# A graph attention kernel: fewer transfers before the first pass, another VectorE order for two blocks, one ScalarE table

The chip is a Trainium2. The program runs on one core of it. The metric is device time in microseconds (us), the median of several executions; executions of one kernel on one chip spread by 3 to 13 us, and by 26 us in the one batch in which two patterns of step 0 are mixed (below).

## The reference, cut to what matters

Two layers work on 4096 nodes with 256 features. Layer 0 is graph attention with four heads; layer 1 takes two steps of top-p attention beside two hops over a dense normalized matrix.

```python
# layer 0
h = jnp.maximum(_layernorm(x), 0.0)
h = (h @ W).reshape(n, heads, head_dim)
e = src[:, :, None] + dst.T[None, :, :]          # src, dst: projections of h per head
e = jnp.where(e > 0, e, ALPHA * e)               # leaky
e = jnp.where(adj[:, None, :] > 0, e, NEG_INF)
out = jnp.einsum('nhm,mhd->nhd', softmax(e), h)  # then a layer norm, and x = x + ...
# layer 1, cut
for n in range(2):
    A = _top_p_attention(Xa, W1, W2, W3)         # softmax, keep the top 0.9 of the mass, renormalize
    Xf = R @ Xf                                  # R = S + I, rows normalized
    Xa = A @ Xa
    Z = Z + Xf @ U1[n].T + Xa @ U2[n].T
```

## The kernel before

Layer 0 starts with a prologue of 32 blocks of 128 nodes. Each block is normalized (`hb`), transposed on TensorE (`tp`, `hT`), multiplied by the weights (`mm`), weighted by two exponentials (`uv`), and split into three bfloat16 parts (`parts`), which go out to DRAM for the later passes. Beside this, GpSimd's queue loads the edges of the first pass. Then 16 passes over pairs of blocks follow, each with sign, masks and products.

```python
            for g in range(NB // 4):
                ...
                rs, nmr = steps(mv, 4, rows)                       # four small GpSimd operations
                for i in range(4):
                    b = 4 * g + i
                    hb = rows.tile([P, D], F32, name="hb")
                    nc.scalar.activation(hb, x4[:, i, :], AF.Relu, scale=rs[:, i:i + 1], bias=nmr[:, i:i + 1])
                    pt = ps2.tile([P, KC, P], F32, name="tp")
                    for k in range(KC):
                        nc.tensor.transpose(pt[:, k, :], hb[:, ts(k, P)], ident)
                    hT = rows.tile([P, KC, P], F32, name="hT")
                    nc.scalar.copy(hT, pt)
                    ...  # two matmuls into pm, two exponentials, two products into uv
                    parts = rows.tile([P, H, 2, W3 + 1], BF16, name="parts", bufs=6)
                    set1 = nc.gpsimd.memset(parts[:, :, :, W3:], 1.0)
                    nc.scalar.copy(parts[:, :, :, :W1], uv)
                    nc.vector.tensor_tensor(uv, uv, parts[:, :, :, :W1], ALU.subtract)
                    if b % 3 == 2 and len(ax) < NB // 4:
                        with tc.issue_after(set1.ins):
                            ax.append(edges(0, len(ax)))           # GpSimd's queue, a load of 1 MB
                    nc.scalar.copy(parts[:, :, :, ds(W1, W1)], uv)
                    nc.vector.tensor_tensor(parts[:, :, :, ds(2 * W1, W1)], uv, parts[:, :, :, ds(W1, W1)], ALU.subtract)
                    nc.gpsimd.tensor_copy(ut0[b // QUARTER][:, b % QUARTER], parts[:, 0])
                    nc.scalar.dma_start(uv_d[:, :, b].rearrange("h p t w -> p h t w"), parts)
            ...
            def signs(k, p):
                g = l0m.tile([P, 2, G0 * P], BF16, name="g", bufs=4)
                ...  # ACT: Relu(BIG * sr + d_big), one per block of the pair
```

In layer 1, each step of attention finds its cut by probes. A probe is a VectorE instruction over 128x4096 that ends in one number per row; a chain of small GpSimd operations on 128x1 turns that number into the next probe's threshold (`lowered`).

```python
            def chosen_kept(b):
                r = blocks[b]
                if 0 < b < NB - 1:
                    second_probe(blocks[b + 1])
                candidates(r, found)
                if b == 0:
                    masked(r)
                ...
                if b + 2 < NB:
                    first_step(blocks[b + 2])
                if b == 0:
                    second_probe(blocks[1])
                if b + 1 < NB:
                    third_probe(blocks[b + 1])
                ...
                if b > 0:
                    masked(r)
```

## Time and profile before

| | kernel before |
|---|---|
| timed executions | 3261.56 us median (3259.44 to 3265.22) |
| the profiled execution | 3278.61 us |
| first row write issued | 31.46 us |
| last row write issued | 143.91 us |
| first sign (start of pass 0) | 151.07 us |
| first masked block of step 0 | 1546.4 us |
| first masked block of step 1 | 2449.4 us |

The profiled execution was 17 us longer than the timed ones. A table of such times, stage by stage, is the way to read a program that is one serial sequence of full stages: a stage that starts earlier passes its gain on unless the next gives it back.

The waits from 27 to 143 us (engine, what waited, for what: us in total, times, longest).

```profile
POOL parts L212 <- DMA uv_d<-parts: 58.1, 17, 7.1
...
ACT parts L218 <- DMA adj_d<-ax: 18.0, 2, 10.4
```

GpSimd waits for row writes to land before it may set the column of ones of a buffer that is used again. ACT is held twice, 18.0 us in all, by writes of edges. The prediction takes a shared semaphore for the reason, and the semaphores recorded in the packed trace agree: the row write issued at 110.40 and an edge write that landed at 110.32 use the same one, and so do the row write issued at 129.25 and an edge write that landed at 129.15.

### The profile page before, as it was taken

To read this page: it belongs to the slowest core of one execution; us is meant where nothing else is said; L and a number is where in the kernel's file an instruction comes from. 1 tells how busy PE (TensorE), PEld (TensorE's weight loads), DVE (VectorE), ACT (ScalarE), POOL (GpSimd) and SP (SyncE) were. 2 spreads that over 40 slices of the span, in tenths; PEclk is the share of its full clock that TensorE was granted. 3 is DMA by queue.
4 is the path that set the end of the run, shared out by engine and by line. 5 is a ranking of instruction groups with operands and counts; after the bars stand their busy time and mean duration, and the time that the engine had idled before them with its cause. 6 is when DMAs were issued, how large, how long until landed. Compare 5 with 4: busy or idle time off the path is not lost. (4 is left out here: it accounts for less than half of the span.)

```text
span 3276.4 us, 51761 instructions
## 1 busy us (share of the span) xinstructions
PE 2973.4 (91%) x19213; PEld 2417.6 (74%) x19213; DVE 2656.6 (81%) x5020; ACT 1952.7 (60%) x2903; POOL 1266.9 (39%) x1793
## 2 busy tenths in 40 slices
PE   4499899898989999986899999999879999999996
PEld 2299799797977888874677777777757777777785
DVE  6598899998976555546999999999469988888894
ACT  5588687786862110016577776775266777776742
POOL 3200100201000000003798998899015656656530
PEclk8699999999999999997899999999889999999998
DMA  9825639356225555520000000000100000000000
GB/s 260 228 83 144 204 113 255 117 142 206 73 85 181 165 177 164 161 89 1 10 19 15 16 20 15 15 18 17 62 13 10 25 20 25 22 22 25 20 27 13
DMA packets 198314, 268.48 MB, mean 82 GB/s; under 512 B 13728, under 2 KB 155552, under 8 KB 198048
## 3 DMA queue, kind: packets, MB, share of 16 engines
q1 hardware_dynamic: 152272, 207.99, 19.4%
q0 software_dynamic: 16896, 33.56, 5.7%
q10 hardware_dynamic: 28880, 23.48, 2.3%
q8 instruction: 155, 2.54, 0.3%
q14 instruction: 111, 0.91, 0.1%
HBM read 226.77 MB, written 71.76 MB: 91 GB/s over the span
## 5 line engine op out<-in xcount | busy, mean ns | idle before, releaser
L799 PE MATMUL acc<-X,eT 128*128 128x256 f32 x4160 | 978.4, 381 | 0.8 <-ACT eT L793 0.8
L799 PEld LDWEIGHTS acc<-X,eT 128*128 128x128 f32 x4160 | 762.6, 191 | 90.1 <-ACT eT L793 1.9
L291 PE MATMUL acc<-ut,m 128*128 128x195 bf16 (+1 forms) x8192 | 732.2, 249 | 82.3 <-DVE m L279 49.7
L291 PEld LDWEIGHTS <-m 128*128 128x128 bf16 x8192 | 703.4, 98 | 111.1 <-DVE m L279 66.9
L272 ACT ACTIVATE g<-sr,d_big 128x1024 bf16<-128x1024 f32 x512 | 550.6, 1178 | 50.2 <-DVE m L278 40.6
L618 ACT ACTIVATE void<-e,c 128x2048 int8<-128x2048 f32 x244 | 490.4, 2010 | 0.6
L611 ACT ACTIVATE e<-mm,nm 128x1024 f32<-128x1024 f32 x256 | 285.9, 1117 | 341.2 <-PE mm L488 338.1
L432 PE MATMUL racc<-hl,ar 128*128 128x512 f32 x2048 | 469.4, 391 | 16.8 <-issue 10.0
L432 PEld LDWEIGHTS racc<-hl,ar 128*128 128x128 f32 x2048 | 384.5, 188 | 101.5 <-issue 10.8
L791 PEld LDWEIGHTS tp<-ident,e 128*128 128x128 f32 x2080 | 246.8, 143 | 224.2 <-issue 126.6
L793 ACT COPY eT<-tp 128x512 f32<-128x512 f32 x520 | 303.4, 584 | 168.9 <-PE tp L791 168.1
L791 PE MATMUL tp<-ident,e 128*128 128x128 f32 x2080 | 327.9, 281 | 57.0 <-DVE e L728 42.8
L278 DVE TENSOR_TENSOR m<-g,ax 128x2048 bf16<-128x2048 bf16 x256 | 311.7, 1218 | 41.8 <-ACT g L272 38.8
L707 DVE MAX8 cand<-big 128x8 f32<-128x228 f32 (+1 forms) x1088 | 343.9, 395 | 0.1
L279 DVE TENSOR_TENSOR m<-ax,m 128x2048 bf16<-128x2048 bf16 x256 | 317.1, 1239 | 26.9 <-DVE m L278 1.4
L488 PE MATMUL mm<-kT,qT 64*128 64x512 f32 x1024 | 304.8, 678 | 33.5 <-ACT e L611 33.5
L428 DVE CAST ar<-at 128x1024 fp32r<-128x1024 bf16 x256 | 177.0, 692 | 169.8 <-PE racc L432 167.3
L694 DVE SCALAR_TENSOR_TENSOR big<-e,lowered 128x4096 f32<-128x4096 f32 x64 | 286.8, 4482 | 20.9 <-POOL lowered L639 20.9
L728 DVE SCALAR_TENSOR_TENSOR e<-e,found 128x4096 f32<-128x4096 f32 x64 | 286.7, 4480 | 0.0
L443 ACT ACTIVATE xf<-xf,rinv 128x256 f32<-128x256 f32 x64 | 32.7, 510 | 373.3 <-DVE xf L442 373.3
L648 POOL TENSOR_TENSOR sums<-sums 128x4 f32<-128x4 f32 (+1 forms) x64 | 106.4, 1662 | 378.8 <-ACT void L618 231.1
L488 PEld LDWEIGHTS mm<-kT,qT 64*128 64x128 f32 x1024 | 84.3, 196 | 130.6 <-issue 66.7
(245 smaller groups left out, 3269.4 us busy)
## 6 DMA issues: line engine op xcount, KB each, us to landing
at<-adj_d SPq DMA_DIRECT2D x256, 256.0 KB, 3.0
ut<-uv_d SPq DMA_DIRECT2D x60, 784.0 KB, 4.3
ax<-in_adj_t_dram POOLq DMA_DIRECT2D x32, 1024.0 KB, 13.6
adj_d<-ax SPq DMA_DIRECT2D x32, 1024.0 KB, 11.5
uv_d<-parts ACTq DMA_DIRECT2D x32, 392.0 KB, 8.2
xf<-xf_d SPq DMA_DIRECT2D x65, 128.0 KB, 2.0
sr<-s_d SPq DMA_DIRECT2D x16, 512.0 KB, 4.7
xf_d<-xf ACTq DMA_DIRECT2D x64, 128.0 KB, 2.4
```

Source lines behind the costliest of these rows:

```text
L272: nc.scalar.activation(g[:, c, :], shared[k].sr, AF.Relu, scale=BIG, bias=d_big[:, h, j:j + 1])
L278: nc.vector.tensor_tensor(m[0], g, a, ALU.min)
L279: nc.vector.tensor_tensor(m[1], a, m[0], ALU.subtract)
L291: nc.tensor.matmul(shared[k].acc[i][:, t, :cols], m[t][:, c, ts(i, P)], shared[k].ut[j // QUARTER][:, j % QUARTER, t, :cols], start=(j == ...
L432: nc.tensor.matmul(acc[i].rearrange("p s d -> p (s d)"), ar[:, c, ts(i, P)], hl[hop][:, j].rearrange("p s d -> p (s d)"), start=(j == 0), ...
L488: nc.tensor.matmul(pm[:, h, :], q[ts(h, DA), :], kT[ts(h, DA), ts(c, 512)], start=True, stop=True)
L618: nc.scalar.activation(void, r.e[:, ts(h, N // 2)], (AF.Relu, AF.Sign)[i], bias=r.c1, scale=-1.0, accum_out=r.sums[:, h, 2 + i:3 + i])
L694: nc.vector.scalar_tensor_tensor(big, r.e, r.c3, r.e, ALU.is_le, ALU.mult, accum_out=r.L)
L707: nc.vector.max(cand[:, s, :], big[:, edges[s]:edges[s + 1]])
L791: nc.tensor.transpose(pt[:, i, :], r.e[:, ts(4 * g + i, P)], ident)
L793: nc.scalar.copy(eT, pt)
L799: nc.tensor.matmul(r.acc[:, 0, :], eT[:, i, :], cur[:, j, :], start=(j == 0), stop=(j == NB - 1))
```

## The change

The intent is to move less by DMA before the first pass, to fill an idle stretch of VectorE at the start of step 0, and to load one ScalarE table for all functions in use.

```diff
+    nc.scalar.preload_act_table_set("natural_log_exp_and_others")
...
+        sr0 = l0.tile([P, G0 * P], F32, name="sr0")
...
-                    if b % 3 == 2 and len(ax) < NB // 4:
+                    if b % 6 == 5:
                         with tc.issue_after(set1.ins):
                             ax.append(edges(0, len(ax)))
...
-                    nc.scalar.dma_start(uv_d[:, :, b].rearrange("h p t w -> p h t w"), parts)
+                    nc.scalar.dma_start(uv_d[1:, :, b].rearrange("h p t w -> p h t w"), parts[:, 1:])
+                    if b % 4 == 3 and b < G0:
+                        pm = ps2.tile([P, 512], F32, name="mm", bufs=3)
+                        for i in range(4):
+                            nc.tensor.transpose(pm[:, ts(i, P)], s_c[:, 0, ds(b - 3 + i, 1)].to_broadcast([P, P]), ident)
+                        nc.scalar.copy(sr0[:, ds((b - 3) * P, 4 * P)], pm)
...
+                if len(ax) < NB // 4:          # after the first masks: the late edge loads
+                    now = small.tile([P, 1], BF16, name="now", bufs=1)
+                    seen = nc.gpsimd.tensor_copy(now, m[0][:, 0, :1])
+                    with tc.issue_after(seen.ins):
+                        while len(ax) < NB // 4:
+                            ax.append(edges(0, len(ax)))
...
-                        sources(0)
-                        shared[0].ut = ut0
+                        shared[0] = SimpleNamespace(sr=sr0, ut=ut0)
...
+                    if k == 0 and p % 4 == 1:
+                        nc.sync.dma_start(uv_d[0, :, ts(p // 4, QUARTER)], ut0[p // 4])
...
-                if 0 < b < NB - 1:
+                early = b < (1 if last else 2)
+                if not early and b < NB - 1:
                     second_probe(blocks[b + 1])
-                candidates(r, found)
-                if b == 0:
+                candidates(r, found, (lambda: second_probe(blocks[b + 1])) if early else None)
+                if early:
                     masked(r)
...
-                if b == 0:
-                    second_probe(blocks[1])
...
-                if b > 0:
+                if not early:
                     masked(r)
```

`candidates` calls its new argument between its sixteen maximum instructions and the small ones after them.

More of the change, by code (lines that the diff above doesn't have):

```diff
@@ L694, in third_probe, with candidates @@
         nc.vector.scalar_tensor_tensor(big, r.e, r.c3, r.e, ALU.is_le, ALU.mult, accum_out=r.L)
-    def candidates(r, found):
+    def candidates(r, found, between=None):
         t, after, eighth = (x[:, r.b:r.b + 1] for x in found)
@@ L707, in candidates @@
             nc.vector.max(cand[:, s, :], big[:, edges[s]:edges[s + 1]])
+        if between:
+            between()
         nc.vector.tensor_scalar(cum[:, :1], r.z, 1.0 - TOP_P, r.L, ALU.mult, ALU.subtract)
```

## The prediction

> **What bounds the kernel now.** I read the page first (busy shares, then the forty slices), then the timeline and the DMA view of the first 160 us, then the waits there, then the timelines where each step of the second layer starts.
>
> From the page, engines and slices (one slice is 81.9 us):
>
> ```profile
> PE 2973.4 (91%) x19213; PEld 2417.6 (74%) x19213; DVE 2656.6 (81%) x5020; ACT 1952.7 (60%) x2903; POOL 1266.9 (39%) x1793
> ...
> PE   4499899898989999986899999999879999999996
> ...
> DMA  9825639356225555520000000000100000000000
> ```
>
> PE is at 8 or 9 tenths nearly everywhere, but at 4 in the first two slices, where DMA is at 9 and 8. So the run is one serial sequence of full stages behind a prologue of some 150 us that does not fill PE. A microsecond saved there is saved at the end.
>
> The timeline of the prologue's end, ACT, DVE and PE (start, duration, what, idle before and its releaser):
>
> ```profile
> 110.81 0.62 ACT L218 CAST parts<-uv 128x520 bf16<-128x520 f32 x1 [10.44 <-DMA adj_d<-ax]
> ...
> 129.66 0.62 ACT L218 CAST parts<-uv 128x520 bf16<-128x520 f32 x1 [7.58 <-DMA adj_d<-ax]
> ...
> 143.91 0.37 ACTq L221 DMA_DIRECT2D uv_d<-parts  x1
> 151.07 29.22 ACT L272 ACTIVATE g<-sr,d_big 128x1024 bf16<-128x1024 f32 x28 [7.82 <-DMA uv_d<-parts]
> 153.34 1.23 DVE L278 TENSOR_TENSOR m<-g,ax 128x2048 bf16<-128x2048 bf16 x1 [9.51 <-ACT g L272]
> ```
>
> Three things are to be seen. ACT is held 10.4 and 7.6 us because its write of a block's rows (uv_d<-parts) shares a completion semaphore with a 1 MB write of edges (adj_d<-ax). The edge writes belong to pass 1 but are issued as soon as a load lands. The last write of rows goes out at 143.91. The first sign ACTIVATE waits until 151.07 **for that write to land**, since its buffer lies where `parts` was. The broadcast row `sr` is not the last thing it waits for: it was issued at 141.2 and such loads took 4.3 to 6.4 us here.
>
> The DMA view from 0 to 151 us (queue, packets, MB, share of sixteen engines):
>
> ```profile
> q0 software_dynamic: 4752, 9.44, 35.3%
> q1 hardware_dynamic: 10976, 17.47, 34.6%
> q10 hardware_dynamic: 17520, 12.99, 28.7%
> ...
> uv_d<-parts ACTq DMA_DIRECT2D x32, 392.0 KB, 8.2
> ax<-in_adj_t_dram POOLq DMA_DIRECT2D x9, 1024.0 KB, 12.7
> adj_d<-ax SPq DMA_DIRECT2D x9, 1024.0 KB, 9.6
> ```
>
> Shares sum to 98.6%, 149 us of work in 151 us: the DMA engines are the prologue's bound. Nine edge loads cost 0.353*151/9 = 5.9 us each, 32 row writes 0.287*151/32 = 1.35 us each.
>
> [...] row writes land after a median 8.2 us under this load, 2.8 us at best. [...] The trace has five loads of 1283 ns. [...] a 0.26 us POOL operation takes 3.99 us behind the 4.48 us probe (second fence below).
>
> **The change, part by part.**
>
> *Prologue DMA.* The instruction order of the changed kernel, as built, has five edge loads before the first sign instead of nine; the other three of pass 0 and the first of the next group follow the first mask. Edge writes issued before then fall from nine to about four and a half. Row writes carry three heads of four; head 0 goes out from the resident `ut` in four 0.8 MB writes, three of them before pass 0. From 40 to 130 us q1 moved 8.37 MB at 25.8% of 90 us, 2.77 us per MB, so 2.9 us per edge write and 2.2 us per `ut` write. Sum: loads -4*5.9 = -23.7, edge writes -4.5*2.9 = -13, rows -0.25*43.3 = -10.8, head 0 +3*2.2 = +6.7: **-41 us of 149**. About 108 us of DMA work remains.
>
> *What then bounds the prologue.* ACT and the chain per block. ACT has hb 0.60, hT 0.37, two exponents 0.23, two casts 1.27 and the DMA issue 0.37; back to back these overlap a little, some 2.55 us a block. The first row write is issued at 31.46, so the 32nd can't be before 31.5 + 31*2.55 = 110.5. Before, the first 22 took 31.46 to 97.43, 3.14 us a block; at that pace with no long holds it would be 128.8. Lighter DMA shortens the landing of row writes, on which the six `parts` buffers turn (POOL's memset waited 58 us for them). I choose 2.8 us a block: 118. The last row write still shares a semaphore with the fifth edge write (I count 0 to 5 us, take 1.5), and the first sign still waits for it to land (three quarters the size, fewer neighbours: 4.5 instead of 7.2). First sign at about 124 against 151.07: **-27 us**. `sr0` made by PE adds eight transposes and two copies (about 1.2 us of ACT, inside this) and, as `sr` wasn't last, gains nothing by itself.
>
> *Pass 0.* It runs at 2.7 us a pair on PE. Late loads are issued near 127 and cost 5.9 us each plus edge writes between them: landed by about 135, 143 and 152. Masks 10, 12 and 14 want them near 152, 157 and 163. No wait, with little room on the last: +0.5.
>
> *One table.* The timeline of step 1's start:
>
> ```profile
> 2413.58 1.28 ACT L554 ACT_TABLE_LOAD   x1 [1.35 <-DVE thr L570]
> 2414.87 0.26 ACT L554 ACTIVATE roots<-roots 128x64 f32<-128x64 f32 x1
> 2415.14 1.28 ACT L555 ACT_TABLE_LOAD   x1
> ...
> 2416.73 0.19 DVE L557 SCALAR_TENSOR_TENSOR nm<-roots,mu 128x32 f32<-128x32 f32 x1 [3.14 <-ACT roots L555]
> ```
>
> Everything after waits for `nm`, so both loads count in step 1: -2.57. In step 0 the first load began at 1500.63, before `var` was ready at 1501.9, so only the second counts: -1.28. The first load of all at 15.0 lay in a wait until 21.5: 0. Sum **-3.8 us**.
>
> *VectorE order.* Only step 0 changes (in the last step the second probe is empty). The timeline there, DVE and POOL:
>
> ```profile
> 1562.73 4.49 DVE L694 SCALAR_TENSOR_TENSOR big<-e,lowered 128x4096 f32<-128x4096 f32 x1 [7.27 <-POOL lowered L639]
> ...
> 1582.81 3.99 POOL L639 TENSOR_SCALAR lowered<-lowered,c 128x1 f32<-128x1 f32 x1
> ```
>
> The intent is to fill the 7.27 us in which DVE waits for POOL's chain (7.1 us). I stepped both engines through their instructions in order with the trace's durations and the rule that POOL stands while a 4.48 us probe runs; that gives every DVE start of the kernel before within 0.4 us. In the new order the third probe of block 1 waits 1.5 instead of 7.3 us, that of block 2 1.5 instead of 0, but the second probe of block 3 now waits 4.1 us for its first step on POOL. Total 7.1 against 7.3 us: from block 2 on DVE is where it was. Step 0 settles to 24.3 us a block on DVE and PE alike (PE's waits for masked `e` sum to 26 us), so block 1's earlier start on PE is not kept: **-0.3 us**.
>
> Sum: -27 + 0.5 - 3.8 - 0.3 = -30.6, so 3261.6 - 30.6 = **3231 us**, -0.9%.
>
> **Rivals.** (1) *The holds remain*: the 21st and 31st row writes share semaphores with edge writes too, and the head-0 writes share them as well. If one or two 5 to 8 us holds stay, the gain is 15 to 20 us: 3243. For it: two such holds cost 18 us before. Against: half as many edge writes. (2) *A new wait in pass 0*: four edge loads at once with their writes between; in pass 3 loads took 9.8 to 25.1 us. At 25 us the third lands at 152 and is just in time[...]. (3) *The order pays in full*: the 7.3 us idle really goes and PE's 10 us earlier start on block 1 is kept, if step 0 were bound by PE: 3224. Against: both engines at 24.3 us. (4) *ACT keeps 2.55 us a block*: 8 us more, 3223.
>
> **Range and chances.** The rivals put -15 to -40 us around -30.6; the runs spread 6 us. Range 3219 to 3244. Two per cent is 65 us, more than the prologue's idle can give (even at the 110.5 floor the gain is about 45): faster 0.02, same 0.97, slower 0.01.
>
> **What would show it.** First sign near 124 (right 118 to 131); no 10 us hold of ACT by adj_d; DMA share before it still above 0.8 but less than 1; the first sign still released by uv_d<-parts; pass 0 without PE gaps at pairs 10 to 14; no table load but one; `nm` 1.3 and 2.6 us closer to `var`; in step 0 a wait of about 4 us of the second probe (block 3) on POOL. It is wrong if holds on semaphores move to other writes, or step 0 keeps the order's gain.

Cuts are marked: the general statements that stood before three measurements (row writes landing in 8.2 us, 2.8 at best; loads of 1283 ns; 0.26 us of GpSimd's work in 3.99 us), and in rival 2 a clause on a late start of the loads with its time, 3238 us, for which no trace stood. The rule by which GpSimd stands while a probe runs rests on those 3.99 us beside a probe of 4.48.

## The result, and the profile after

The changed kernel took **3243.95 us** (3240.59 to 3246.96, four runs) beside 3262.10 us for the kernel before (3259.44 to 3265.22, four runs). The ratio is 0.9944, with a 95% interval of 0.9927 to 0.9961: the same at 2%, 18 us faster. A ratio here is the mean time of one kernel's fast runs over the mean of the other's in the same rounds, so it is not quite the ratio of the medians quoted. The median lies 0.05 us inside the predicted range of 3219 to 3244, at its slow end, and two of the four executions lie outside: that it falls inside is luck. The gain was 18 us and not 31.

The changed kernel's page, engines and slices:

```profile
PE 2964.9 (92%) x19221; PEld 2414.3 (75%) x19221; DVE 2656.1 (82%) x5020; ACT 1945.4 (60%) x2901; POOL 1156.8 (36%) x1794
...
PE   4699898898989999986899999999879999999996
...
DMA  7937539465235555520000000000200000000000
```

The second slice of PE went from 4 to 6 tenths and the first of DMA from 9 to 7. The rest of the sequence has hardly moved. The timeline of ACT at the end of its prologue:

```profile
126.77 0.37 ACTq L225 DMA_DIRECT2D uv_d<-parts  x1
134.21 29.22 ACT L282 ACTIVATE g<-sr,d_big 128x1024 bf16<-128x1024 f32 x28 [8.31 <-DMA uv_d<-ut]
```

The last row write is issued at 126.77 and the first sign starts at 134.21, 16.9 us sooner than before. The sign starts 7.4 us after the issue. The profile names the head-0 write, `uv_d<-ut`, as the releaser, but that one was issued at 127.36 and landed 7.5 us later, when the sign had begun. The last row write landed at 133.95, after 7.2 us, and ACT's wait for its semaphore ended then: the sign waited for the last row write, as forecast.

The DMA view of the changed kernel, 0 to 143 us (queue, packets, MB, share of sixteen engines; then KB each and the median us from issue to landing):

```profile
q1 hardware_dynamic: 9440, 16.48, 33.6%
q0 software_dynamic: 2812, 5.60, 24.1%
q10 hardware_dynamic: 13424, 9.78, 22.0%
...
uv_d<-parts ACTq DMA_DIRECT2D x32, 294.0 KB, 4.5
```

The shares sum to 79.7%, against 98.6 before (the forecast was above 80). A share near 1 does not say that the engines are full: for 60 to 90 and 90 to 120 us the view by windows gives 1.08 and 1.10 before, and the changed kernel still has 1.05 from 90 to 120. Row writes land in a median 4.5 us, against 8.2. Yet the row writes, 31 intervals from 30.62 to 126.77 us, still go out every 3.10 us. Before, that number was 3.63 us with the two holds in it, and (112.45 - 18.0) / 31 = 3.05 us without them. So the prologue gained about what the two holds cost (the last issue is 17.1 us sooner), and its pace, the mean time from one row write to the next, did not fall.

The wait of `nm` at the start of step 0 in the kernel before; then that start in the changed kernel, ACT and DVE, where the table loads were, and `nm` of its step 1:

```profile
1503.79 0.19 DVE L557 SCALAR_TENSOR_TENSOR nm<-roots,mu 128x32 f32<-128x32 f32 x1 [1.80 <-ACT roots L555]
```

```profile
1483.15 0.26 ACT L572 ACTIVATE roots<-roots 128x64 f32<-128x64 f32 x1 [1.31 <-DVE roots L571]
1483.44 0.26 ACT L573 ACTIVATE roots<-roots 128x64 f32<-128x64 f32 x1
1483.73 0.19 DVE L575 SCALAR_TENSOR_TENSOR nm<-roots,mu 128x32 f32<-128x32 f32 x1 [0.53 <-ACT roots L573]
...
2379.79 0.19 DVE L575 SCALAR_TENSOR_TENSOR nm<-roots,mu 128x32 f32<-128x32 f32 x1 [0.86 <-ACT roots L573]
```

No load stands between the logarithm and the exponential. In step 0 `nm` waits 0.53 us instead of 1.80, in step 1 0.86 instead of the 3.14 in the prediction's lines: 1.27 and 2.28 us less, where 1.28 and 2.57 were forecast. In the prediction's lines a load took 1.28 us and the activation began 0.01 us after it (load at 2413.58, activation at 2414.87); the second load started at 2415.14, 0.01 us after the end of the activation before it. The new VectorE order in step 0 of the changed kernel, DVE's timeline:

```profile
1536.01 4.49 DVE L712 SCALAR_TENSOR_TENSOR big<-e,lowered 128x4096 f32<-128x4096 f32 x1 [1.36 <-POOL lowered L657]
...
1561.65 4.48 DVE L712 SCALAR_TENSOR_TENSOR big<-e,lowered 128x4096 f32<-128x4096 f32 x1 [1.36 <-POOL lowered L657]
...
1569.93 4.49 DVE L691 SCALAR_TENSOR_TENSOR junk<-e,lowered 128x4096 uint8<-128x4096 f32 x1 [3.79 <-POOL lowered L657]
```

Waits of 1.4, 1.4 and 3.8 us stand where one of 7.27 stood. The prediction had stepped them out as 1.5, 1.5 and 4.1.

### The profile page after: what moved, and what is told of

It is laid out like the page before. It is cut to its first block, busy times and chain, and to the rows that moved or that the text cites. A ratio compares the mean times of both kernels' runs of the same rounds, so it can differ in the third digit from the quotient of the medians.

```text
span 3238.8 us, 51773 instructions
## 1 busy us (share of the span) xinstructions
PE 2964.9 (92%) x19221; PEld 2414.3 (75%) x19221; DVE 2656.1 (82%) x5020; ACT 1945.4 (60%) x2901; POOL 1156.8 (36%) x1794
## 5 line engine op out<-in xcount | busy, mean ns | idle before, releaser
L282 ACT ACTIVATE g<-sr,d_big 128x1024 bf16<-128x1024 f32 x512 | 550.7, 1180 | 50.5 <-DVE m L288 40.4
L506 PEld LDWEIGHTS mm<-kT,qT 64*128 64x128 f32 x1024 | 83.8, 195 | 126.1 <-issue 67.1
```

Source lines behind the costliest of these rows:

```text
L282: nc.scalar.activation(g[:, c, :], shared[k].sr, AF.Relu, scale=BIG, bias=d_big[:, h, j:j + 1])
L506: nc.tensor.matmul(pm[:, h, :], q[ts(h, DA), :], kT[ts(h, DA), ts(c, 512)], start=True, stop=True)
```

## The experiments

Twelve runs follow, ten of them of edited kernels, in three batches on three chips; every result was correct, and each that was timed is the same at 2%. Kernels of one batch share the runs of the kernel before. A pace or a first sign comes from one trace each: the unaltered changed kernel, traced twice, gave 3.10 and 3.12 us and 134.2 and 136.0 us.

### First batch: each part alone

**The kernel before, unaltered**, with no edit.

> The kernel before, unchanged, as its own rival: ratio 1.000 within 0.2% by any theory. What is asked of its profile: are VectorE's waits of 0.6 us on POOL in step 0 (19 times, 11.7 us, and a period of 24.4 or 25.1 us a block) there in every execution, or only in the one profiled first (3276 us, while the timed runs took 3259 to 3265)? If they belong to the kernel, the profile shows them again; if they are an accident of one execution, the period is 24.4 us throughout and the span near 3260.

It took 3259.26 us; ratio 0.9988 (0.9972 to 1.0003). First sign at 151.4 us, as in the first trace. Of the waits of 0.6 us it has none, so they belong to some executions and not to the kernel (more below).

**The VectorE order alone**, put on the kernel before:

```diff
+                early = b < (1 if last else 2)
-                candidates(r, found)
+                candidates(r, found, (lambda: second_probe(blocks[b + 1])) if early else None)
```

> The kernel before with only the new VectorE order of step 0's first blocks. My step-through: -0.3 us, ratio 0.9999, because the wait that goes from block 1's third probe comes back at block 3's second probe. Rival: POOL gets ahead by the new order and the repeated 0.6 us waits of step 0 vanish with it, -5 to -12 us, ratio 0.9965 to 0.9985. The profile: period of the masked instruction in step 0 24.4 us throughout if the rival holds.

It took 3259.27 us; ratio 0.9999 (0.9985 to 1.0012). Block 1 is masked at 1572.0 us, against 1589.7 in the control, 17.6 us sooner. But this trace was already 4.5 us ahead when the projections of step 0 began (1447.5 against 1452.0) and 3.1 us at block 0, and it is 7.9 us ahead at block 2 and 5.9 at block 30: of the lead at block 1, 1.4 to 2.8 us are left. The forecast of nearly nothing holds, and the rival of 5 to 12 us falls.

**The table alone:**

```diff
+    nc.scalar.preload_act_table_set("natural_log_exp_and_others")
```

> The kernel before with only the one ScalarE table. Mine: -3.8 us (one load of 1.28 us off step 0's chain, two off step 1's), ratio 0.9988. Rival: the loads hide and nothing comes of it, ratio 1.000. The profile: no table load after the first, roots to nm 0.5 us instead of 1.8 and 3.1.

It took 3253.64 us; ratio 0.9982 (0.9968 to 0.9996), that is -5.9 us with a half-width of 4.6. The forecast of -3.8 lies inside. In this execution's trace the first sign came at 149.3 instead of 151.4, with 14.7 us of holds by edge writes instead of the control's 17.3, so part of the 5.9 may not be the table's.

**The transfers alone** (edges, row writes of three heads, head 0 later, `sr0`):

```diff
-                    if b % 3 == 2 and len(ax) < NB // 4:
+                    if b % 6 == 5:
-                    nc.scalar.dma_start(uv_d[:, :, b].rearrange("h p t w -> p h t w"), parts)
+                    nc.scalar.dma_start(uv_d[1:, :, b].rearrange("h p t w -> p h t w"), parts[:, 1:])
```

> The kernel before with only the first pass's part of the change (edges, rows, head 0, broadcast row made by PE). The trace of the changed kernel puts the first sign at 134.2 instead of 151.1: -17 us, ratio 0.9948, if all of it reaches the end. Rival: part of it is given back in pass 0 or later, -10 us or less, ratio 0.997 or more.

It took 3248.11 us; ratio 0.9960 (0.9947 to 0.9974), -13 us; the interval holds the forecast, 0.9948, and the rival's 0.997 too. First sign at 136.2 us, 15.2 sooner than the control; a row write every 3.21 us, although no hold by an edge write is left. The three parts sum to 0.01 + 0.18 + 0.40 = 0.59%, and the whole change measured 0.56%: they add up, and the transfers, forecast at -27 us before the first sign, are the part that fell short.

### Second batch: why the pace stayed at 3.1 us

For each of three theories, a run takes away one thing that could set the pace; a fourth run takes away the landing of the last writes.

**DMA: one edge load in the prologue instead of five.**

```diff
-                    if b % 6 == 5:
+                    if b == 5:
```

> The changed kernel with one edge load in the prologue of layer 0 instead of five; the other seven are asked for after the first masks (pass 0 then waits for them, so the whole time is not the point). Forecast of the record's step: the block pace is set by the DMA work, so with 4 x 2.1 MB less the row writes go out every 2.8 us or less, landings take 2 to 3 us, and the first sign starts at 122 to 127 us (134.2 in the changed kernel). Rival (half-clock TensorE, or the one-at-a-time chain of a block): the pace stays 3.0 to 3.2 us and only the landing of the last write shortens, first sign at 129 to 132 us.

One execution: 3259.37 us (pass 0 waits for its edges, as said). The window from 60 to 120 us (busy us of PE, PEld, DVE, ACT and POOL, then TensorE's clock, DMA share and GB/s), first of the changed kernel, then of this one:

```profile
60.00:120.00 60.00, 37.04 (x118) 23.02 (x116) 42.85 (x99) 41.38 (x117) 23.42 (x56) 0.76 0.97 271
```

```profile
60.00:120.00 60.00, 37.51 (x121) 24.01 (x119) 42.07 (x98) 41.10 (x117) 23.59 (x49) 0.76 0.46 153
```

The DMA share fell from 0.97 to 0.46, the median landing of a row write from 4.5 to 2.5 us, and every engine did the same amount of work in the window. The pace is 3.11 us. The first sign came at 133.25, later than either theory had it, since the last row write took 5.4 us to land. **The DMA load does not set the pace.** That rejects the step on which the forecast of 2.8 us rested.

**TensorE's clock: three useless matmuls a block**, into a PSUM bank that nobody reads.

```diff
                         nc.tensor.transpose(pt[:, k, :], hb[:, ts(k, P)], ident)
+                    warm = ps2.tile([P, 512], F32, name="warm", bufs=1)
+                    nc.tensor.matmul(warm[:, :D + 2 * H], hb[:, :P], wx[:, 0, :], start=True, stop=True)
...
+                    for k in range(2):
+                        nc.tensor.matmul(warm[:, :D + 2 * H], hT[:, k, :], wx[:, 0, :], start=True, stop=True)
```

In the changed kernel's trace the four products of a block take 2.13 us where the granted clock is 0.50 and 1.16 us where it is 1.00.

> The changed kernel with three matmuls of no use added to each block of the prologue (one while the copy of the transposed rows runs, two after the products), into a PSUM bank that nobody reads, so that TensorE idles less and is granted its full clock more. Theory 'half clock': the granted clock of the prologue rises from 0.5 to 0.8 to over 0.9, the four products take 1.16 us in nearly all blocks, and the pace falls from 3.1 us to 2.6 to 2.8, first sign at 120 to 126 us. Rivals (DMA or GpSimd waits): the clock rises but the pace stays 3.0 to 3.2, first sign 133 to 138 us.

One execution: 3237.36 us. The same window:

```profile
60.00:120.00 60.00, 53.92 (x237) 41.72 (x235) 42.35 (x98) 41.55 (x117) 20.69 (x51) 0.97 0.92 260
```

The clock rose from 0.76 to 0.97, DVE and ACT did the same work in the window, and the pace is 3.12 us. The half clock is in the trace, and it isn't what sets the pace either. The first sign came at 131.3 us, sooner than the rivals' 133 to 138, because the landing of the last write was shorter (3.2 us). It is one execution, and its trace has none of the waits of the slower pattern (below) in which the kernel before ran in this batch, so the 3237 us is no verdict.

**GpSimd's queue: the column of ones set once, in six kept buffers.**

```diff
+            turn6 = [l0w.tile([P, H, 2, W3 + 1], BF16, name=f"parts{i}") for i in range(6)]
+            for t in turn6:
+                set1 = nc.gpsimd.memset(t[:, :, :, W3:], 1.0)
...
-                    parts = rows.tile([P, H, 2, W3 + 1], BF16, name="parts", bufs=6)
-                    set1 = nc.gpsimd.memset(parts[:, :, :, W3:], 1.0)
+                    parts = turn6[b % 6]
...             # the first edge load now comes at the start, the others after the copies of ut, at blocks 6, 12, 18 and 24
```

> The changed kernel with six kept row buffers whose column of ones is set once at the start, so that GpSimd no longer waits in its queue for a row write to land before it may set that column. Theory 'GpSimd head of line': the 5 to 8 us waits of GpSimd for the row writes go, [...] pace 2.8 us or less, first sign 120 to 127 us, whole time 5 to 10 us under the changed kernel. Rival (DMA latency through six buffers): the same waits move to the ScalarE copy into the buffer, the pace stays 3.1, first sign 132 to 136 us, whole time within 3 us of the changed kernel.

(The changed kernel's waits from 27 to 143 us have none of VectorE for GpSimd.)

The waits from 27 to 135 us, first of the changed kernel (to 143 us), then of this one:

```profile
POOL parts L216 <- DMA uv_d<-parts: 34.8, 14, 7.8
```

```profile
POOL ut L225 <- DVE parts L224: 58.8, 29, 5.6
```

GpSimd's waits for row writes are gone; it now waits for the block's own VectorE result, which is where it stands in the chain. The pace is 3.12 us. The first sign came at 130.9, sooner than in the changed kernel, not through the pace: it still waited for the last row write, which landed after 2.6 us instead of 7.2. 3246.92 us, ratio 0.9912 (0.9897 to 0.9927) to a kernel before of 3276.78 in this batch. The changed kernel was not run in it, so what was expected of the whole time against the changed kernel is not settled, for this run and the next.

**The landing of the last writes: the last two blocks' buffers kept.**

```diff
+        tail = [l0.tile([P, H, 2, W3 + 1], BF16, name=f"tail{i}") for i in range(2)]
-                    parts = rows.tile([P, H, 2, W3 + 1], BF16, name="parts", bufs=6)
+                    parts = rows.tile([P, H, 2, W3 + 1], BF16, name="parts", bufs=6) if b < NB - 2 else tail[b - NB]
-                g = l0m.tile([P, 2, G0 * P], BF16, name="g", bufs=4)
+                g = l0m.tile([P, 2, G0 * P], BF16, name="g", bufs=3)
```

> The changed kernel with the last two blocks' row buffers in memory that layer 0 keeps (and three sign buffers in place of four, to make room), so the first sign's memory no longer waits for the last two row writes to land. Theory 'landing of the last write': the first sign starts some 5 us sooner, near 129 us, and the whole time falls by 4 to 6 us against the changed kernel. Rival: three sign buffers cost what is won, or another wait takes its place (head-0 write, the last constants): within 2 us.

The timeline of ACT there:

```profile
125.64 0.37 ACTq L226 DMA_DIRECT2D uv_d<-tail  x1
126.33 14.66 ACT L283 ACTIVATE g<-sr,d_big 128x1024 bf16<-128x1024 f32 x14 [1.46 <-POOL ut L225]
```

The first sign starts 0.7 us after the last write was issued: 7.9 us sooner than in the changed kernel, more than forecast. The profile names a computation as its releaser; the write `s_d<-sT` landed at the same time, 126.18. Some of the gain is lost again in the passes, with three sign buffers (the signs' waits for masks rose from 40.4 to 93.2 us): the last sign lies at 918.8 instead of 923.6, so 4.8 us are left. 3244.05 us, ratio 0.9903 (0.9888 to 0.9918).

### A second pattern of step 0

In the second batch the kernel before ran at 3273 to 3284 us in nine of ten executions and at 3258 in one. The clocks agree (0.955 to 0.960), so it is not the clock. The traces tell the two apart: the masked blocks of step 0 come every 24.4 us in the control's trace, and every 25.1 us for 19 of the blocks in the first trace of the kernel before and for 19 and 20 in the last two kernels above. So the first two traces must not be subtracted: their spans differ by 37.6 us, the timed runs by 18. The third batch began with a test of this.

**The changed kernel again:**

> The changed kernel unaltered, as the yardstick of this batch. Two readings are tested. First, the last batch's kernel before ran at 3277 us in 9 of 10 executions and at 3258 in one, and the two variants of the changed kernel that were profiled there show 18 and 19 waits of 0.6 us of VectorE for GpSimd in step 0 (12 us). If that slow pattern belongs to the chip, the changed kernel shows it on such a chip too (3244 becomes 3255 to 3258 there, and the ratio to the kernel before stays 0.993 to 0.996); if the new VectorE order protects from it, it stays at 3241 to 3247 beside a kernel before of 3277. On a chip without the pattern: 3241 to 3247 beside 3261. Second, first sign again near 134 us, last row write near 127.

It took 3255.47 us beside a kernel before of 3277.87 us; ratio 0.9934 (0.9921 to 0.9948), that is -22.4 us. Both are in the slow pattern by their times; the new order does not protect from it. First sign at 136.0 us, last row write at 128.2, some 2 and 1 us later than forecast. DVE's waits in step 0 of this execution:

```profile
DVE junk L691 <- POOL lowered L657: 11.0, 18, 0.6
```

Both patterns stand side by side in its trace; here is the end of one slow period and of one fast one, first POOL's timeline, then DVE's.

```profile
1841.04 4.85 POOL L656 TENSOR_TENSOR lowered<-inv_e,a 128x1 f32<-128x1 f32 x1
1846.00 0.26 POOL L657 TENSOR_SCALAR lowered<-lowered,c 128x1 f32<-128x1 f32 x1
...
1866.10 0.56 POOL L656 TENSOR_TENSOR lowered<-inv_e,a 128x1 f32<-128x1 f32 x1
1866.76 3.93 POOL L657 TENSOR_SCALAR lowered<-lowered,c 128x1 f32<-128x1 f32 x1
```

```profile
1841.00 4.48 DVE L748 SCALAR_TENSOR_TENSOR e<-e,found 128x4096 f32<-128x4096 f32 x1
...
1846.30 4.49 DVE L691 SCALAR_TENSOR_TENSOR junk<-e,lowered 128x4096 uint8<-128x4096 f32 x1 [0.61 <-POOL lowered L657]
...
1866.06 4.50 DVE L748 SCALAR_TENSOR_TENSOR e<-e,found 128x4096 f32<-128x4096 f32 x1
...
1870.73 4.49 DVE L691 SCALAR_TENSOR_TENSOR junk<-e,lowered 128x4096 uint8<-128x4096 f32 x1
```

In each period GpSimd has two small operations left when VectorE starts a 4.48 us instruction. In the fast period the first slips in (0.56 us) and the last is held until VectorE ends (3.93 us, to 1870.69; VectorE's instruction to 1870.56); the next probe starts at once. In the slow period the first is held (4.85 us, to 1845.89; VectorE's to 1845.48), and the last, 0.26 us of work, comes after; the probe waits 0.61 us for it. The prediction's fence has such a hold too, 3.99 us for the same operation. What decides which operation is held is not shown: in both periods GpSimd's start is recorded 0.04 us after VectorE's. Eighteen such waits are 11 us, the difference between the changed kernel's two medians (3255.47 and 3243.95); the kernel before differs by 16.8 between the batches, of which the 19 waits of its first trace would account for 11.7. By times and traces most executions of these two batches had the slow pattern (of eight traces, the kernel with useless matmuls alone has none of the waits, that with one edge load has three), and in the first batch's traces there is none. Why one chip or execution falls into it stays open.

### Third batch: combinations

**Kept last buffers and useless matmuls** (the two edits above):

> Kept row buffers for the last two blocks and three matmuls of no use a block. In the runs so far the useless matmuls alone gave a pace of 3.12 us a block (3.20 without) and the full clock, the kept buffers alone a first sign at 126.3. If TensorE's half clock is one of two causes that hide each other, the pace stays 3.05 to 3.15 here, first sign 124 to 127 us, whole time 6 to 10 us under the changed kernel of the same chip and state.

(Its 3.20, and the 3.23 in the next text, divide by 30 intervals; by 31 they are 3.10 and 3.12.) 3251.08 us, ratio 0.9922 (0.9909 to 0.9936); pace 3.11 us, as expected; first sign 128.7 us, later than expected: it now waits for `s_d<-sT`, which landed at 128.51. It is 4 us under the changed kernel, not 6 to 10.

**Kept last buffers and ones set once:**

> Kept row buffers for the last two blocks, and the column of ones set once (no GpSimd wait for row writes). Alone the latter left the pace at 3.23 us. Expected: pace 3.15 to 3.25, first sign 125 to 128, whole time 5 to 8 us under the changed kernel of the same chip and state.

**3244.45 us** (3241.72 to 3247.14, four executions), ratio 0.9902 (0.9886 to 0.9917); pace 2.94 us, lower than expected and the lowest of all; first sign 125.7 us. ACT there:

```profile
122.17 0.37 ACTq L230 DMA_DIRECT2D uv_d<-tail  x1
125.71 5.30 ACT L287 ACTIVATE g<-sr,d_big 128x1024 bf16<-128x1024 f32 x5 [4.11 <-DMA uv_d<-parts]
```

The first sign waits again, 3.5 us after the last issue, now for the row write of the third block from the end, which was issued at 118.16 and took 7.4 us: two kept buffers were not enough here. It was run beside the changed kernel at 3255.47 us, both in the slow pattern (21 and 18 waits of 0.6 us), so it is 11 us faster than the changed kernel, more than the 5 to 8 expected, and 33 us faster than the kernel before. It beats both kernels: its interval and the changed kernel's, 0.9921 to 0.9948, do not meet.

**All three:**

> All three: kept row buffers for the last two blocks, ones set once, three useless matmuls a block. Theory 'two causes that hide each other' (half-clock products and GpSimd's waits for row writes, each taking the place of the other when one is removed): only here the pace falls, to 2.6 to 2.9 us a block, last row write 112 to 120 us, first sign 113 to 121 us, whole time 12 to 20 us under the changed kernel. Rival 'the order in which four in-order engines hand a block to each other': the pace stays 3.0 to 3.2 and the first sign 123 to 127 us, whole time as in the run with the kept buffers alone.

3248.20 us, ratio 0.9916 (0.9903 to 0.9930); pace (125.18 - 30.96) / 31 = 3.04 us, first sign 126.1 us. This is what the rival had, in pace and first sign. The clock is 1.00 in the window, and the waits of this trace, from 27 to 130 us, name no DMA but one wait of 1.7 us before the first sign; the DMA share is still 0.96. The pace is still not 2.8, so the half clock and GpSimd's waits do not hide each other. (A run that takes the DMA load away too was not made; no engine waits for it here.) What is left, by elimination and not shown by a run of its own, is how a block is handed from engine to engine in fixed orders (while ACT's row write waited in the kernel before, from 100.4 to 110.4 us, ACT ran nothing else): ACT writes `hb`, TensorE transposes, ACT copies, TensorE multiplies, VectorE and ACT alternate over `uv` and `parts`, GpSimd copies. In the changed kernel's window none of them is full (DVE 71%, ACT 69%, PE 62% of 60 us; ACT's twenty row-write issues of 0.37 us, which the busy time leaves out, bring it to 81%), so each idles for another. Which hand-over to shorten stays open. So does why the pace was 2.94 without the useless matmuls and 3.04 with them, and 3.21 with the transfers alone.

## Why the prediction was right, and where it was not

| step | forecast | measured |
|---|---|---|
| last row write issued | 118 + 1.5 = 119.5 us | 126.8 us |
| from there to the first sign | 4.5 us | 7.4 us |
| first sign | 124 us (-27) | 134.2 us (-16.9) |
| first sign to first hop | +0.5 us | 814.6 us against 815.0 in the control |
| one table | -3.8 us | -5.9 +- 4.6 us |
| VectorE order | -0.3 us | ratio 0.9999 +- 0.0014 |
| sum | -30.6 us | -18 us; -22 in the slow pattern |

**The failed step is "I choose 2.8 us a block: 118".** The pace measured 3.10 us, and 0.3 us times 31 is 9.3 us of the miss of 10.2 us at the first sign. The landing adds 2.9; against that, the first row write went out 0.8 us sooner and the 1.5 us taken for a shared semaphore did not arise. The reason given for 2.8, that lighter DMA shortens the landing of row writes and with it the pace, is refuted: with half the DMA share and a landing of 2.5 us the pace was 3.11. The sentence under the DMA view, "the DMA engines are the prologue's bound", drew a bound from a high share; what the runs showed in its place is a pace that stayed at 3.11 to 3.12 us when the DMA load, the half clock or GpSimd's waits were taken away one at a time, and at 2.94 to 3.11 in the combinations. What does set it stays open. The better number was in the same paragraph: 3.14 us a block without the holds, and a last write at 128.8; it was issued at 126.8.

**The landing** was a mis-sized term: 7.2 us for the last row write, not 4.5. The median did fall to 4.5, but the last write lands slower than the median. Edges are not the reason: the last edge write had landed at 123.44, and none was in flight at 126.77. Just before it, at 125.67 and 126.04, two loads of `sr` of 512 KB each go out, which pass 0 no longer needs. In the eight traces where they go out before the last row write or with it (within 0.05 us), it took 5.1 to 7.6 us to land; in the six where they follow, 2.6 to 3.2 in five and 5.1 in one. That order was not tested by a run of its own. Keeping two buffers removed this term in one run, which shows that the first sign waited for it; in the run with ones set once, an earlier row write took its place.

**The holds** went: no wait of ACT for `adj_d` is left in the changed prologue. Removing them would account for the prologue's gain, 18.0 us of holds against 17.1 us at the last issue; no run took them away alone, so that match is an argument. It is looser in the run of the transfers alone: the control had 17.3 us of holds, and the last issue came 13.1 us sooner, as the pace was 3.21. Rival 1 named the right time, 3243 us, for a wrong reason: no hold stayed.

**Right as told:** pass 0 had no gap. From 150 to 185 us the waits show none of PE, and DVE's are waits for PE, at most 0.5 us each. The late loads went out at 139 to 141 us, not near 127, since they follow the first mask at 136.5; the three that pass 0 needs landed at 147.6, 153.5 and 161.4, and masks 10, 12 and 14 came at 162.4, 167.9 and 173.4. The table gain agrees within its interval, and `nm` no longer waits for loads. The order moved 7.3 us of idle time into 1.4, 1.4 and 3.8 us and was worth nothing. The row of sources was not the last thing waited for; it was not tested alone.

**Not foreseen:** the second pattern of step 0. The prediction used the first trace's step 0 as typical; it was in the slow pattern. As both kernels of the first comparison and of the third batch ran in the same pattern, by their times, the comparison of timed runs is little touched, but a comparison of two single executions is.

## What to carry to other kernels

A high DMA share over a stage does not show that DMA sets its pace: take the intervals between a regular marker (here the row writes), set the long holds apart from the rest, and forecast only what removes a hold, unless a run with less traffic shows the pace itself moving (here the share fell from 0.97 to 0.46 and the pace stayed, 3.10 and 3.11 us a block). A row write that shared a semaphore with a 1 MB edge write held ACT for 10.4 and 7.6 us here. A higher TensorE clock bought nothing in this prologue: 0.97 instead of 0.76, and 3.12 us a block against 3.10. When the next stage's buffer lies over memory that is still being written out, keeping the last buffers elsewhere can save the landing of the last write; here 7.9 us at the first sign in one run, of which 4.8 were left at the last sign, while in another an earlier write still held the sign for 3.5 us. Before two traces are subtracted, check that a stage the change doesn't touch has the same period in both.
